# A routed mixture of experts on one core: seven single tiles for eight, an earlier index table, and third tiles in column groups

## The chip, the cores and the metric

The kernel runs on one core of one Trainium2 chip. The metric is the device time of one execution in microseconds (us), taken as the median of several runs; lower is better.

## The reference

There are 64 x 64 = 4096 tokens of 256 numbers. Each token goes to two of eight experts, and the experts' outputs, scaled by softmax weights, are added to the token. Cut to what matters:

```python
var = jnp.mean(x * x, axis=-1, keepdims=True)
xn = rms_w * (x * jax.lax.rsqrt(var + EPS))
gate = xn @ wg_W + wg_b + (genre_embed @ gg_W + gg_b)        # [64, 64, 8]
gate_w = jax.nn.softmax(gate, axis=-1)
topk_w, topk_i = jax.lax.top_k(gate_w, 2)
cw = jnp.sum(jax.nn.one_hot(topk_i, E) * topk_w[..., None], axis=-2)
h1 = jax.nn.relu(jnp.einsum('bsh,ehm->bsem', x, W1) + b1)     # 256 -> 512
h2 = jax.nn.relu(jnp.einsum('bsem,emn->bsen', h1, W2) + b2)   # 512 -> 512
out_e = jnp.einsum('bsen,enh->bseh', h2, W3) + b3             # 512 -> 256
x = x + jnp.einsum('bseh,bse->bsh', out_e, cw)
```

All is float32. The kernel computes only the two chosen experts of each token: 8192 pairs of token and expert.

## The kernel before

**Two routings.** A token's number is 32 p + i; the tokens with i under 8 (`NA`, 1024 tokens) are the first part. `first_part` finds their experts early. Each expert's first 128 pairs of this part form a *single*, a tile of 128 rows, units u = 0 to 7 (`E`). While the singles run, the generator `rest` routes all else: it counts for every expert how many pairs are left (`mm`), gives each its tiles of 128 rows (`nb_i`) and its number of blocks of 32 rows (`ints`), chooses the shape of the tail, and computes for each row of the rest which token it holds. That last step is a table: VectorE builds one-hot matrices in four chunks (L774, L776, L779, the buffers `ohl`, `ohh`, `ohv`), and 64 small matmuls in float16 (`table`, L613) add them up in PSUM bank 7; from it VectorE makes the indices `idxR` (L785 to L788). `gather_unit` then lets GpSimd gather the rows of x for the first two units of the rest.

**The rest's units.** A unit holds up to four tiles of one expert; its width counts blocks of 32 rows, at most 16. `SHAPES` lists 32 tails (q, p, widths) that the program holds as separate code: q units of width 16, then the experts' last units, of which p come with a unit of width 8 behind them. At the run the first listed shape that fits is jumped to; if none fits, a general one. For the inputs here, by the counts of the reference's routing, it is (5, 6, (15, 14, 12, 11, 11, 10, 16, 9)): five units of 16, then 16, 9, 15, 8, 14, 8, 12, 8, 11, 8, 11, 8, 10, 8. Expert 7 has 300 pairs in the first part and 945 behind it; with 128 in its single, 1117 are left, 35 blocks.

**How a unit is computed.** A single runs `layer1` (L1043, 8 matmuls), `layer2` (L1053, 16) and `layer3` (L1290, 4 of 256 columns), each float32 matmul showing as two records. Units of more than one tile use a fast scheme with seven products in place of eight (`Fast` for layers 1 and 2, L1152; `Wide` for layer 3, L1254), named p(1) to p(7); VectorE makes the sums (`mix`, `c11`, `c12`, `c22`) and ScalarE copies and relus. Layer 3 in that scheme takes tiles by twos, so a unit of three tiles computes its third tile's layer 3 with plain matmuls (L1290), whatever its number of rows.

**The order.** It is written by hand; engines work their instructions in the order of the program, waiting on semaphores. `head_step(u)` is the order around single u: layer 1 of u, the transposes of u + 1, layer 3 of u - 1, layer 2 of u, and calls of `more(ns)`, which put some of the rest's routing at that place. `step` does the same for the last single, and `step_fast` for the units of the rest: layers 1 and 2 of unit u with the end of layer 2 and layer 3 of unit u - 1 between them. `give(u)` scales the result on VectorE (L1321) and adds the rows into the output with a scatter on GpSimd (L1322); a unit's scatters wait until those of the unit before have landed. The output is filled with x ahead of that by four copies (`fill`, SP's queue). `pB.spread` makes the weights of the second routing on GpSimd (L432 to L434) and stores them in DRAM (`cwdR`, L435), `gather_cw` gathers them for a unit (`cg`), and `scales` copies the expert's column (`cw`, L1014). The weights come from DRAM on SP's queue: `load_weights` for the singles' layers 1 and 3 (rings of three buffers, `w1r` and `w3r`) and all experts' layer 2 (`w2a`), `stream_1` and `stream_3` for the rest's units.

Of the kernel before, what the change touches and what calls it, by code (L numbers as in the profile page):

```python
# [58 lines left out]
def kernel(  # L59
# [38 lines left out]
    NREST = (NPAIR - TOPK * BT + E * (BT - 1)) // BT  # L98
    NSURE = (NPAIR - E * BT) // BT
# [515 lines left out]
    def rest():  # L615
# [41 lines left out]
        V.tensor_tensor(totA, totA1[:, 1:], totA1[:, 0:E], ALU.subtract)  # L657
        V.tensor_scalar(more, totA, float(-BT), 0.0, ALU.add, ALU.max)
# [73 lines left out]
        V.scalar_tensor_tensor(pA.slot, pA.slot, float(-BT), pA.along(base), ALU.add, ALU.add)  # L732
        for k, sum_ in enumerate((place, turn_e)):
# [1007 lines left out]
```

## Time and profile before

| what | value |
| --- | --- |
| median of 3 runs | 451.8 us (451.03 to 452.44) |
| the profiled execution | 451.29 us, its span 449.6 us |
| TensorE (PE) busy | 440.6 us, 98% of the span |
| VectorE (DVE) busy | 358.3 us, 80% |
| ScalarE (ACT) busy | 258.3 us, 57% |
| GpSimd (POOL) busy | 274.7 us, 61% |
| read from and written to memory | 56.34 MB and 20.12 MB |

The span runs from the first to the last instruction. A row of a timeline gives start and duration in us, engine, line, operation, output and input tile, the shapes and how many in a row; in brackets stands how long the engine stood idle before it and what ended that. Matmuls overlap, so what a group of them costs is read from its start to the start of the next, not from its duration. The singles run from 22 to 87 us, the units of the rest behind that.

### The profile page before, as it was taken

Reading aid. Unit: us, or ns where it says so; the run is one execution under the profiler, and the core shown is the slowest. Engines: PE = TensorE matmul, PEld = TensorE weight load, DVE = VectorE, ACT = ScalarE, POOL = GpSimd, SP = SyncE. Lnnn points to the kernel's source line nnn. Section 1 sums busy time; section 2 is a strip of 40 time slices with the busy share of each in tenths; the row PEclk is TensorE's granted clock in tenths of the full one; section 3 lists DMA queues with packets and bytes.
Section 4 is the critical chain, followed back from the end, with each engine's and each line's share of the span. In section 5 each row is a group of like instructions: output and inputs, shape, how many; then the busy total and the mean of one; then the engine's idle time right before and its main releaser. Section 6 shows DMA issues by size and latency. Waiting matters only on the chain.

```text
span 449.6 us, 9495 instructions
## 1 busy us (share of the span) xinstructions
PE 440.6 (98%) x3092; PEld 414.6 (92%) x3092; DVE 358.3 (80%) x988; ACT 258.3 (57%) x618; POOL 274.7 (61%) x234
## 2 busy tenths in 40 slices
PE   8899999999999999999999999999999999999994
PEld 7689999988989899999999899999999999999994
DVE  5797995677798888888899877977977878779851
ACT  6755543456465555646475655755755765666642
POOL 4355522857888875737475864874775766667333
PEclk9999999999999999999999999999999999999998
DMA  8799999794666757545654563474464565555213
GB/s 292 277 330 372 378 372 383 279 251 91 186 158 150 164 87 195 94 115 106 145 117 100 92 156 96 68 166 106 66 163 108 124 132 117 123 107 105 25 16 41
DMA packets 71599, 72.51 MB, mean 161 GB/s; under 512 B 34735, under 2 KB 60818, under 8 KB 71156
## 3 DMA queue, kind: packets, MB, share of 16 engines
q1 hardware_dynamic: 48976, 43.29, 30.9%
q0 software_dynamic: 14960, 17.50, 23.0%
q10 hardware_dynamic: 7604, 11.02, 7.9%
q8 instruction: 26, 0.43, 0.4%
q14 instruction: 33, 0.27, 0.2%
HBM read 56.34 MB, written 20.12 MB: 170 GB/s over the span
## 4 chain that ended last, share of the span: by engine, by line
PE 90%; DMA 3%; DVE 2%; issue 1%; POOL 1%; POOLq 0%; SPq 0%; DVEq 0%
PE pb L1152 54%; PE pb L1254 18%; PE pb L1053 6%; PE pb L1290 5%; PE pb L1043 3%; DMA big<-in_x_dram 2%; POOL out_dram L1322 1%; PE pb L613 1%; PE pb L934 1%; DMA xg<-in_x_dram,idxA 1%; PE pb L253 1%; DVE xT L922 0%; DVE big L1129 0%; POOLq L1641 0%; PE pb L271 0%
## 5 line engine op out<-in xcount | busy, mean ns | idle before, releaser
L1322 POOL DMA_INDIRECT out_dram<-ys,idxR x57 | 98.8, 1732 | 81.7 <-DVE ys L1321 64.1
L1152 PE MATMUL pb<-hid,big 128*128 128x256 f32 (+7 forms) x456 | 83.0, 325 | 0.0
L1173 ACT ACTIVATE hid<-hid,bb 128x256 f32<-128x256 f32 (+12 forms) x154 | 72.9, 523 | 12.6 <-DVE hid L1167 12.3
L867 POOL DMA_INDIRECT cg<-cwdR,idxR x59 | 64.0, 1085 | 18.0 <-issue 17.7
L1152 PEld LDWEIGHTS pb<-hid,big 128*128 128x128 f32 x456 | 70.4, 191 | 3.4
L1161 ACT COPY big<-pb 128x512 f32<-128x512 f32 (+7 forms) x57 | 27.2, 477 | 64.8 <-PE pb L1152 46.6
L1152 PE MATMUL pb<-mixB,big 128*128 128x256 f32 (+7 forms) x304 | 55.5, 325 | 0.1
L1152 PE MATMUL pb<-hotA,big 128*128 128x256 f32 (+7 forms) x304 | 55.3, 325 | 0.0
L1152 PEld LDWEIGHTS pb<-mixB,big 128*128 128x128 f32 x304 | 47.9, 191 | 3.1 <-ACT bc L1031 0.5
L1152 PEld LDWEIGHTS pb<-hotA,big 128*128 128x128 f32 x304 | 46.6, 191 | 2.1
L1152 PE MATMUL pb<-mixX,iotx 128*128 128x256 f32 (+7 forms) x228 | 46.5, 327 | 0.0
L867 POOL DMA_INDIRECT big<-in_x_dram,idxR x32 | 36.0, 1124 | 9.8 <-issue 8.5
L867 POOL DMA_INDIRECT xgE<-in_x_dram,idxR x27 | 30.9, 1145 | 16.1 <-issue 15.2
L1152 PEld LDWEIGHTS pb<-mixX,iotx 128*128 128x128 f32 x228 | 36.6, 191 | 2.9 <-issue 0.8
L1161 ACT COPY q1s<-pb 128x512 f32<-128x512 f32 (+7 forms) x57 | 26.9, 472 | 19.0 <-PE pb L1152 17.6
L1275 DVE TENSOR_TENSOR ys<-pb,big 128x128 f32<-128x128 f32 (+1 forms) x54 | 18.7, 347 | 22.3 <-PE pb L1254 15.4
L1263 ACT COPY big<-pb 128x128 f32<-128x128 f32 (+1 forms) x54 | 16.7, 309 | 25.9 <-PE pb L1254 25.9
L1053 PEld LDWEIGHTS pb<-hid,w2a 128*128 128x128 f32 x256 | 29.8, 192 | 1.1 <-issue 0.8
L1152 PE MATMUL pb<-xT,w1r 128*128 128x256 f32 (+7 forms) x152 | 30.8, 325 | 0.0
L1053 PE MATMUL pb<-hid,w2a 128*128 128x128 f32 x256 | 30.5, 276 | 0.0
L922 DVE STREAM_TRANSPOSE xT<-gTs 128x256 f32<-128x256 f32 x55 | 29.3, 638 | 0.5 <-DMA gTs<-scr 0.5
L1031 ACT ACTIVATE bc<-b_sb,cw 128x256 f32 x59 | 26.1, 499 | 6.1 <-DVE cw L1014 5.0
(340 smaller groups left out, 925.5 us busy)
## 6 DMA issues: line engine op xcount, KB each, us to landing
w2a<-in_L_cond_W_dram SPq DMA_DIRECT2D x8, 1024.0 KB, 13.2
w1r<-in_L_cond_W_dram SPq DMA_DIRECT2D x11, 512.0 KB, 11.5
w3r<-in_L_cond_W_dram ACTq DMA_DIRECT2D x11, 512.0 KB, 3.9
w3r<-in_L_cond_W_dram SPq DMA_DIRECT2D x10, 512.0 KB, 12.9
w1r<-in_L_cond_W_dram ACTq DMA_DIRECT2D x10, 512.0 KB, 3.8
gTs<-scr SPq DMA_DIRECT2D x7, 512.0 KB, 4.3
out_dram<-in_x_dram SPq DMA_DIRECT2D x4, 768.0 KB, 9.5
scr<-big SPq DMA_DIRECT2D x5, 512.0 KB, 4.3
```

Of the source, the lines that this page charges most:

```text
L867: return nc.gpsimd.indirect_dma_start(out=dst, out_offset=None, in_=src, in_offset=bass.IndirectOffsetOnAxis(ap=index(b), axis=0), bounds_ ...
L922: V.transpose(xT[:, :, s0 + k, :].rearrange("p c (b k) -> p k c b", b=SQ), shs[:, s0 + k].rearrange("p k (a c) -> p k c a", a=SQ),)
L1031: nc.scalar.mul(bc, b3e, cw)
L1053: nc.tensor.matmul(ph, lhsT=w2[:, m, ts(n, P)], rhs=hid[0][:, m, 0:BT], start=(m == 0), stop=(m == MC - 1))
L1152: nc.tensor.matmul(bank[:, ts(n, self.w)], lhsT=w[:, c, ts(n, P)], rhs=x[:, c], start=new and n == 0 and c == 0, stop=n == HB - 1 and c == ...
L1161: nc.scalar.copy(self.q[(1, 6, 5).index(k)], self.tall(self.X if k == 5 else self.U))
L1173: nc.scalar.activation(out, src, AF.Relu, bias=ww[self.u][1][:, self.l, n : n + 1])
L1254: nc.tensor.matmul(bank[:, ts(j, H // 2)], lhsT=a[:, c, ts(j, P)], rhs=b[:, c], start=new and j == 0 and c == 0, stop=j == self.n - 1 and ...
L1263: nc.scalar.copy(self.q[(1, 6, 5).index(k)], self.X if k == 5 else self.U)
L1275: V.tensor_tensor(self.y(j, i), src, self.q[q].rearrange("p (k h) -> p k h", k=self.n), ALU.add)
L1290: nc.tensor.matmul(sums(u, k)[0 : cols.stop - cols.start], lhsT=hid[1][:, n, cols], rhs=w3[:, n, :], start=(i == 0), stop=(i == MC - 1),)
L1322: add = nc.gpsimd.indirect_dma_start(out=orows, out_offset=bass.IndirectOffsetOnAxis(ap=index(b)[0:n], axis=0), in_=y[0:n], in_offset=None ...
```

## The change

`F = 7` takes the place of `E` where singles are counted. Expert 7 has no single: its pairs of the first part go into the rest, so it has 1245 pairs there, 39 blocks, and the shape chosen is (5, 6, (15, 15, 14, 12, 11, 10, 16, 9)), from a new list. Its layer 1 and layer 3 weights are no longer loaded for a single. The table's last matmuls, the indices and the gathers come one single earlier, ahead of layer 2 of single 5, and all that follows them moves with them. A third tile of at most 64 rows (`strip`) puts its four products into column groups of TensorE, side by side on PSUM's partitions (`third_tile`), and adds the groups with a matmul against a 0/1 matrix (`join`; `both`, and `four` for 32 rows). `r1`, a relu on ScalarE, moves behind the third tile.

The diff, cut to its core (the other places only put `F` for `E`; of the 32 shapes the one that is used is shown):

```diff
 SHAPES = [
-    (5, 6, (15, 14, 12, 11, 11, 10, 16, 9)),
+    (5, 6, (15, 15, 14, 12, 11, 10, 16, 9)),
...
-    NREST = (NPAIR - TOPK * BT + E * (BT - 1)) // BT
-    NSURE = (NPAIR - E * BT) // BT
+    F = 7
+    NREST = (NPAIR - max(F - E + TOPK, 0) * BT + E * (BT - 1)) // BT
+    NSURE = (NPAIR - F * BT) // BT
...
-        V.tensor_tensor(totA, totA1[:, 1:], totA1[:, 0:E], ALU.subtract)
-        V.tensor_scalar(more, totA, float(-BT), 0.0, ALU.add, ALU.max)
+        V.tensor_tensor(more, totA1[:, 1:], totA1[:, 0:E], ALU.subtract)
+        V.tensor_scalar(more[:, 0:F], more[:, 0:F], float(-BT), 0.0, ALU.add, ALU.max)
...
-        V.scalar_tensor_tensor(pA.slot, pA.slot, float(-BT), pA.along(base), ALU.add, ALU.add)
+        V.tensor_scalar(low, pA.slot[:, 0:F], float(BT), float(-4 * NPAIR - BT), ALU.is_lt, ALU.mult)
+        V.tensor_tensor(pA.slot, pA.slot, pA.along(base), ALU.add)
...
+        V.scalar_tensor_tensor(pA.slot[:, 0:F], pA.slot[:, 0:F], float(-BT), low, ALU.add, ALU.add)
...
-        V.tensor_tensor(sl[:, :, 0:NA], sl[:, :, 0:NA], low, ALU.add)
...
     def sums(u, k):
 
         if size(u) == 3 and k == 2:
-            return PB[2][:, 0:H]
+            return PB[2][:, H : 2 * H] if strip(u) and u not in ends else PB[2][:, 0:H]
...
+    def strip(u):
+
+        rows = width(u) - 2 * BT
+        return rows if size(u) == 3 and rows <= BT // 2 else 0
+
+    def third_tile(u):
+
+        r = strip(u)
+        if not r:
+            layer3(u, [2])
+            return
+        w3, c0 = ww[u][3], 2 * BT
+        ways = P // r
+        for n in range(MC):
+            q = n % ways
+            nc.tensor.matmul(
+                PB[2][q * r : (q + 1) * r, 0:H],
+                lhsT=hid[1][:, n, c0 : c0 + r],
+                rhs=w3[:, n, :],
+                start=n < ways,
+                stop=n >= MC - ways,
+                skip_group_check=True,
+            )
+        nc.scalar.copy(ring(run, [P, H], "xg", 3, 0), PB[2][:, 0:H])
+
+    def join(u):
+
+        r = strip(u)
+        if r:
+            fold = both if r == BT // 2 else four
+            nc.tensor.matmul(PB[2][0:r, H : 2 * H], lhsT=fold, rhs=ring(run, [P, H], "xg", 3, 0), start=True, stop=True)
...
     def head_step(u, more):
...
-        table(GC * (NCH - 1) * (u == E - 2))
         layer1(u)
         if u + RING < E:
-            load_weights(u + RING, (0, 1))
+            load_weights(u + RING, (0, 1) if u + RING < F else (1,))
...
-            if u == E - 2:
-                while not fetched:
-                    more(1000000)
+            if u == F - 2:
+                more(1000000)
             elif u != 2:
                 more(3200)
             scaled(u - 1, "A")
             layer3(u - 1)
...
-        table(GC * (u == E - 3))
+        table(GC * (u == F - 2))
...
-        if u == E - 2:
-            stream_3(E, mybir.EngineType.SP)
+        if u == F - 2:
             fill(2)
-            stream_1(E + 1, mybir.EngineType.SP)
-            stow(E + 1)
-            shuffle(E + 1)
-            fill(3)
             give(u - 2)
-        if u >= 1 and u != E - 3:
+        if u >= 1 and u != F - 3:
             give(u - 1)
...
     def step(u, last):
 
         far = fetches_of(u, last)
+        if u == F - 1:
+            while not fetched:
+                next(other)
+            stream_3(F, mybir.EngineType.SP)
+            stream_1(F + 1, mybir.EngineType.SP)
+            stow(F + 1)
+            shuffle(F + 1)
+            fill(3)
...
+        if u == F - 1:
+            for _ in other:
+                pass
...
-            elif u + 1 == E:
-                for l in (1, 0):
-                    for _ in Fast(E, l).fold():
+            elif u + 1 == F:
+                for l in (0, 1):
+                    for _ in Fast(F, l).fold():
                         pass
...
             third.p(1)
-            f.r1()
             third.p(2)
             if n == 3:
-                layer3(u - 1, [2])
+                third_tile(u - 1)
+            f.r1()
...
             if n == 3:
+                join(u - 1)
                 give(u - 1, [2])
...
-        for u in range(E - 1):
+        for u in range(F - 1):
             head_step(u, routing)
-        for _ in other:
-            pass
-        for u in range(E - 1, CUT):
+        V.tensor_tensor(four, both[:, 0 : P // 4], both[:, P // 4 : P // 2], ALU.add)
+        for u in range(F - 1, CUT):
```

What this moves, engine by engine. On TensorE, around the end of single 5 (`xT` and `w1r` layer 1, `w2a` layer 2, `w3r` layer 3, `pb_75<-big` the table; the table's rows repeat 16 times a chunk and are cut), before:

```order
L1043 MATMUL pb_71<-xT,w1r_84 128x128 x2
L934 MATMUL pb_72<-ident,xg_205 128x128 x2
L1290 MATMUL pb_73<-w3r_87,hid_91 128x256 x4
L613 LDWEIGHTS big
L613 MATMUL pb_75<-big 128x69
...
L1053 MATMUL pb_68<-hid_90,w2a 128x128 x4
```

And now:

```order
L1043 MATMUL pb_71<-xT,w1r_84 128x128 x2
L934 MATMUL pb_72<-ident,xg_205 128x128 x2
L615 LDWEIGHTS big
L615 MATMUL pb_75<-big 128x70
...
L1322 MATMUL pb_73<-w3r_87,hid_91 128x256 x4
...
L1053 MATMUL pb_68<-hid_90,w2a 128x128 x4
```

Before, 16 of the table's matmuls stand between layer 3 of single 4 and layer 2 of single 5, and 48 further down (32 ahead of layer 1 of single 6, 16 behind it). Now 16 stand ahead of that layer 3 and the other 48 behind it, all ahead of layer 2 of single 5.

On GpSimd, from the last gathers of singles (`xg`) to the first weights of the rest (`cg`); `out_dram` is a `give`'s scatter, before:

```order
L867 DMA xg_206<-in_x_dram,idxA 128x256
L1322 DMA out_dram<-ys,idxA 4096x256
L867 DMA xgE<-in_x_dram,idxR 128x256 x4
L867 DMA big<-in_x_dram,idxR 128x256 x4
L802 COPY cw8B<-cw8A 128x64
...
L435 DMA cwdR<-cw8B 128x256
L1322 DMA out_dram<-ys,idxA 4096x256
L1322 DMA out_dram<-xg_207,idxA 4096x256
L867 DMA cg<-cwdR,idxR 128x8 x4
L1322 DMA out_dram<-xg_205,idxA 4096x256
```

And now:

```order
L1354 DMA out_dram<-ys,idxA 4096x256
L867 DMA big<-in_x_dram,idxR 128x256 x4
L867 DMA xgE<-in_x_dram,idxR 128x256 x4
L1354 DMA out_dram<-ys,idxA 4096x256
L1354 DMA out_dram<-xg_206,idxA 4096x256
L802 COPY cw8B<-cw8A 128x64
...
L437 DMA cwdR<-cw8B 128x256
L867 DMA cg<-cwdR,idxR 128x8 x4
L1354 DMA out_dram<-xg_207,idxA 4096x256
```

The scatters of singles 3 and 4, of which the first stood ahead of the gathers and the second behind the store of `cwdR`, now both stand between the gathers and the copy that begins the spread; the `cg` gathers come right behind the store.

On VectorE, at the routing's one-hot chunks (`big<-iotx`, `big<-whole`, `big<-big,xgE`), before:

```order
L774 TENSOR_TENSOR big<-iotx,lo_854 128x2048
L776 TENSOR_TENSOR big<-whole,hi_855 128x1104
L779 TENSOR_TENSOR big<-big,xgE 128x1104
L1321 SCALAR_TENSOR_TENSOR ys<-pb_74,cg,bc_574 128x256
L774 TENSOR_TENSOR big<-iotx,lo_854 128x2048
```

And now:

```order
L779 TENSOR_TENSOR big<-big,xgE 128x1120
L785 TENSOR_SCALAR sa<-pb_75 128x70
...
L795 SCALAR_TENSOR_TENSOR nex<-ia,fit,ib 128x1
L1353 SCALAR_TENSOR_TENSOR ys<-pb_74,cg,bc_574 128x256
L1353 SCALAR_TENSOR_TENSOR xg_206<-pb_73,cg,bc_571 128x256
```

The `give` of single 3 stood between the first two chunks and now stands behind the indices, beside that of single 4.

More of the change, by code (lines that the diff above doesn't have):

```diff
@@ L169 @@
     nc.gpsimd.tensor_tensor(both, ident[:, 0 : P // 2], ident[:, P // 2 : P], ALU.add)
+    four = const.tile([P, P // 4], F32, name="four")
     fresh = const.tile([P, NB, E], F32, name="fresh")
@@ L644, in rest @@
         place, turn_e = t2("place", 1), t2("turn_e", 1)
+        sl, low = buf(gx, [P, TOPK, NI], "sl"), buf(gx, [P, F, NA], "low")
         flat = pin.rearrange("p a k e -> p a (k e)")
@@ L788, in rest @@
         V.tensor_tensor(idxR, sa, sb, ALU.add)
-        gather_unit(E)
-        gather_unit(E + 1)
+        gather_unit(F)
+        gather_unit(F + 1)
         total, ia, ib = ends[:, KE - 1 : KE], t2("ia", 1), t2("ib", 1)
@@ L830, in width @@
     def width(u):
-        return BT if u < E else SQ * plan[u - E][1]
+        return BT if u < F else SQ * plan[u - F][1]
     def group(u):
-        return u if u < E else E + plan[u - E][2]
+        return u if u < F else F + plan[u - F][2]
     def follow(u):
-        return u > E and group(u) == group(u - 1)
+        return u > F and group(u) == group(u - 1)
     def size(u):
@@ L845, in tiles @@
     def tiles(u):
-        b = u if u < E else E + plan[u - E][0]
+        b = u if u < F else F + plan[u - F][0]
         return list(range(b, b + size(u)))
     def turn_of(u, k):
-        return (u if u < E else E + sum(size(v) for v in range(E, u))) + k
+        return (u if u < F else F + sum(size(v) for v in range(F, u))) + k
     def within(u, k):
@@ L862, in index @@
     def index(b):
-        return idxA[:, b : b + 1] if b < E else idxR[:, b - E : b - E + 1]
+        return idxA[:, b : b + 1] if b < F else idxR[:, b - F : b - F + 1]
     def fetch(dst, src, b):
@@ L895, in gather_cw @@
             cg = cgs[b] = cgR[:, turn_of(u, k) % NCG]
-            fetch(cg, (cwdA if b < E else cwdR)[:, :], b)
+            fetch(cg, (cwdA if b < F else cwdR)[:, :], b)
     xT = buf(run, [P, HC, SLOTS, BT], "xT")
@@ L932, in transpose_x @@
             for k, b in enumerate(bs):
-                g = ring(run, [P, H], "xg", 3, b) if u < E else xgR[u % 2][:, k]
+                g = ring(run, [P, H], "xg", 3, b) if u < F else xgR[u % 2][:, k]
                 nc.tensor.transpose(tps[c][:, ts(k, BT)], g.rearrange("p (r c) -> p c r", c=HC)[:, c], ident)
-            if u == E:
+            if u == F:
                 (nc.scalar.copy if c else V.tensor_copy)(
@@ L985, in streams @@
     def streams(u, end):
-        if E < u + 2 < end and not follow(u + 2):
+        if F < u + 2 < end and not follow(u + 2):
             stream_1(u + 2)
-        if E < u + 1 < end and not follow(u + 1):
+        if F < u + 1 < end and not follow(u + 1):
             stream_3(u + 1)
     def stage_1(u):
-        if u < E:
+        if u < F:
             ww[u] = [w1r[u % RING], vT[:, :, u, :], w2a[:, u], w3r[u % RING]]
@@ L1019, in scaled @@
         cws = []
-        e = expert(u, mybir.EngineType.Activation) if eng == "A" and u >= E else ex.get(u)
+        e = expert(u, mybir.EngineType.Activation) if eng == "A" and u >= F else ex.get(u)
         for k, b in enumerate(tiles(u)):
@@ L1330, in give @@
             )
-            if b < E:
+            if b < F:
                 for f in fills[1:]:
-                    tc.declare_no_dep(add.ins, f.ins, reason="the first E tiles hold tokens of the first part alone")
+                    tc.declare_no_dep(add.ins, f.ins, reason="the first F tiles hold tokens of the first part alone")
             behind = list(adds[-2]) if len(adds) > 1 else [fills[0]]
-            if b >= E and not behind_fills:
+            if b >= F and not behind_fills:
                 behind += fills[1:]
@@ L1358, in head_step @@
     def head_step(u, more):
-        if u + 3 < E:
+        if u + 3 < F:
             gather(u + 3)
-        for k in range(3 * u, min(3 * u + 3, E)):
+        for k in range(3 * u, min(3 * u + 3, F)):
             gather_cw(k)
-        table(GC * (NCH - 1) * (u == E - 2))
         layer1(u)
         if u + RING < E:
-            load_weights(u + RING, (0, 1))
+            load_weights(u + RING, (0, 1) if u + RING < F else (1,))
         if u == 0:
@@ L1410, in fill @@
         for a in sum(adds, []):
-            tc.declare_no_dep(f.ins, a.ins, reason="the first E tiles hold tokens of the first part alone")
+            tc.declare_no_dep(f.ins, a.ins, reason="the first F tiles hold tokens of the first part alone")
         fills.append(f)
     def fetches_of(u, last):
-        far = E + 1 < u + 2 < last
+        far = F + 1 < u + 2 < last
         if far:
@@ L1431, in step @@
         if len(ww[u - 1]) < 5:
-            if u - 1 >= E:
+            if u - 1 >= F:
                 scales(u - 1)
@@ L1456, in step @@
         layer3(u - 1)
-        if u == E - 1:
-            stream_1(E + 2, mybir.EngineType.SP)
-            stream_3(E + 1, mybir.EngineType.SP)
+        if u == F - 1:
+            stream_1(F + 2, mybir.EngineType.SP)
+            stream_3(F + 1, mybir.EngineType.SP)
         give(u - 1)
     def step_fast(u, last):
-        if u == E:
+        if u == F:
             transpose_x(u)
@@ L1473, in step_fast @@
         n = size(u - 1)
-        e = expert(u, mybir.EngineType.Activation) if u > E and not follow(u) else None
+        e = expert(u, mybir.EngineType.Activation) if u > F and not follow(u) else None
         fresh_w, fold_next = not follow(u), fast_next and not follow(u + 1)
-        if u == E:
+        if u == F:
             layer3(u - 1, part=(0, 1))
@@ L1573, in step_fast @@
             shuffle(u + 2)
-        small = u > E
+        small = u > F
         if small:
@@ L1653, in steps @@
                 nc.gpsimd.drain()
-    CUT = E + NQT - 2
+    CUT = F + NQT - 2
     ENGS = (
@@ L1706 @@
         plan[:] = ARMS[k]
-        last = E + len(plan)
+        last = F + len(plan)
         with tc.manual_schedule():
```

38 lines of the change are left out of this document (17 added, 21 removed), and 60 rows, old and new, of the table SHAPES.

## The prediction

> **What bounds the kernel now.** I read the page first, then who waits for whom on TensorE, then the timelines of TensorE, VectorE and GpSimd around the places that the change touches.
>
> ```profile
> span 449.6 us, 9495 instructions
> PE 440.6 (98%) x3092; PEld 414.6 (92%) x3092; DVE 358.3 (80%) x988; ACT 258.3 (57%) x618; POOL 274.7 (61%) x234
> ```
> ```profile
> PE pb L481 <- DVE ones L158: 1.1, 1, 1.1
> PE pb L253 <- DMA big<-in_x_dram: 0.8, 1, 0.8
> PE pb L934 <- DMA xg<-in_x_dram,idxA: 0.6, 1, 0.6
> ```
>
> The first fence is the page's head, the second all that TensorE waits for: 2.5 us, all before 22 us. So TensorE (PE) is the bound: its work counts in full, and every wait put into its queue counts in full. The question is whether the shorter head puts waits there.
>
> **The single that goes.** The last single's layers stand undisturbed in TensorE's timeline (start, duration; from one start to the next is what a group costs):
>
> ```profile
> 63.27 0.40 PE L934 MATMUL pb<-ident,xg 128*128 128x128 f32 x2
> 63.51 1.89 PE L1290 MATMUL pb<-w3r,hid 128*128 128x256 f32 x8
> 65.24 1.14 PE L613 MATMUL pb<-big 128*128 128x69 f16 x16
> 66.20 3.82 PE L1053 MATMUL pb<-hid,w2a 128*128 128x128 f32 x32
> ...
> 80.27 1.95 PE L1043 MATMUL pb<-xT,w1r 128*128 128x128 f32 x16
> 82.06 1.89 PE L1290 MATMUL pb<-w3r,hid 128*128 128x256 f32 x8
> 83.78 3.73 PE L1053 MATMUL pb<-hid,w2a 128*128 128x128 f32 x32
> 87.36 1.12 PE L934 MATMUL pb<-ident,xgE 128*128 128x128 f32 x8
> ```
>
> Layer 1 costs 82.06 - 80.27 = 1.79, layer 3 83.78 - 82.06 = 1.72, layer 2 87.36 - 83.78 = 3.58, and a single's transposes 63.51 - 63.27 = 0.24: 7.33 us less. Its weights' loads (1 MB for layers 1 and 3), its gathers and its scatter lay beside other work and no wait hung on them: nothing.
>
> **The rows that come back.** Expert 7's 128 pairs of the first tokens now join its rest: 1117 pairs become 1245, 35 blocks of 32 become 39. Its last unit grows from width 11 to 15, and the units run 15, 8, 15, 8, 14, 8, 12, 8, 11, 8, 10, 8 where they ran 15, 8, 14, 8, 12, 8, 11, 8, 11, 8, 10, 8. One "11 and 8" becomes a "15 and 8". Layer 1 of a unit begins with these rows; half the width in elements is the moving side (224 is width 14, 192 is 12, 176 is 11), and the next two are from the grouped view, mean ns of one:
>
> ```profile
> 283.41 0.92 PE L1152 MATMUL pb<-xT,w1r 128*128 128x224 f32 x4
> 318.06 0.82 PE L1152 MATMUL pb<-xT,w1r 128*128 128x192 f32 x4
> 349.07 0.76 PE L1152 MATMUL pb<-xT,w1r 128*128 128x176 f32 x4
> 378.95 0.76 PE L1152 MATMUL pb<-xT,w1r 128*128 128x176 f32 x4
> ```
> ```profile
> L1152 PE MATMUL pb<-hid,big 128*128 128x240 f32 x24 | 5.4, 366 | 0.0
> L1152 PE MATMUL pb<-hid,big 128*128 128x224 f32 x24 | 5.0, 353 | 0.0
> ```
>
> "14 and 8" takes 318.06 - 283.41 = 34.65, "11 and 8" 378.95 - 349.07 = 29.88. From 14 to 15 each of the 84 records (7 products x 2 x 3 matmuls, two records each) takes 366 - 353 = 13 ns more, 1.10 us; layer 3 is the same for four tiles. So 15 and 8 is 35.75, and the change adds 5.87 us. The additional tile's gather, scale and scatter run on GpSimd, 61% busy: nothing, as long as that engine keeps ahead; behind they would cost 1 to 2 us each.
>
> **Column groups.** Third tiles of 32 and 64 rows (the units of width 9 and 10) put their four products beside each other and sum them in one more matmul. The nearest rows are four matmuls of 512 columns in groups of 32, which the gates already do, and the third tile of 32 rows as it is:
>
> ```profile
> 25.11 1.46 PE L284 MATMUL pb<-big,wg_sb 128*32 128x512 f32 x8
> 26.51 0.71 PE L1053 MATMUL pb<-hid,w2a 128*128 128x128 f32 x4
> ```
> ```profile
> 252.42 1.91 PE L1290 MATMUL pb<-w3r,hid 128*32 128x256 f32 x8
> 254.27 1.08 PE L1152 MATMUL pb<-mixX,iotx 128*128 128x240 f32 x4
> ```
>
> One after another, four of 512 columns would take 2 x 1.73 = 3.46 us (63.51 to 65.24 is four of 256); they took 1.40, so groups do run together: two passes of 0.43 and 0.54 for going in and out of the narrow shape. With 256 columns that is 0.43 + 0.54 = 0.97 for four groups and 0.86 + 0.54 = 1.40 for two. The sum over groups is one matmul of 256 columns, 1.73 / 4 = 0.43, and 0 to 0.54 for the shape again. Width 9 goes from 1.85 to between 1.40 and 1.94; width 10, one after another now at some 1.85 too, to between 1.83 and 2.37. Together -0.5 to +0.6; I take -0.3, nearer to the lower end because the narrow tile pays for its shape today as well, partly ahead of the 1.85. The Trainium skill (TensorEngine Tiling (Array Packing), Overview) gives up to 4x for 32 rows and 2x for 64; by that the two third tiles with their sums would take 0.86 and 1.29, and the change would be worth 1.5 us here, 1.2 more than I take. The same page's section Tiling Modes says that a change of mode drains the array, which the 0.54 of this trace bears out. The later relu (`r1`, now behind the third tile) stays on ScalarE, 57% busy: nothing.
>
> So TensorE's work changes by -7.33 + 5.87 - 0.3 = -1.76 us. Now the waits.
>
> **First wait: the table.** The 64 one-hot matmuls that give the rest's indices stood 16 behind layer 3 of single 4, 32 before layer 1 of single 6, 16 behind it. Now all stand before layer 2 of single 5. VectorE makes their operands without a pause from 46 us on:
>
> ```profile
> 61.13 0.48 DVE L1321 SCALAR_TENSOR_TENSOR ys<-pb,cg,bc 128x256 f32<-128x256 f32 x1
> 61.53 1.21 DVE L774 TENSOR_TENSOR big<-iotx,lo 128x2048 f16<-128x2048 f16 x1
> ...
> 70.24 0.73 DVE L779 TENSOR_TENSOR big<-big,xgE 128x1104 f16<-128x1104 f16 x1
> 75.09 0.23 DVE L785 TENSOR_SCALAR sa<-pb 128x69 f32<-128x69 f32 x1 [4.12 <-PE pb L613]
> 75.76 0.23 DVE L788 TENSOR_TENSOR idxR<-sa,sb 128x69 int32<-128x69 f32 x1
> ```
>
> The last operand ends at 70.97. One `give` (61.13 to 61.53) moves behind it: 70.57; the other edits of the routing (a wider `low`, one operation less, 1120 columns for 1104) cancel to 0.1. TensorE reaches the last 16 early: transposes done at 63.51, 16 table matmuls 0.96, layer 3 1.73, 32 more 1.92, so 68.1. It waits until 70.6, some 2.5 us. Before, VectorE waited there (4.12). TensorE then reaches the rest's first transposes at 87.36 - 7.33 + 2.5 = 82.5, 4.8 us earlier than now. The indices come 3.3 us earlier (70.6 + 1.14 = 71.8 where 75.09 stood), so the gathers that those transposes need have 1.5 us less of their cover; nothing in the trace waits there now, and I put up to 0.5 us on it, which the next wait swallows. On SP's queue the rest's first weights and the copies of x to the output go out about a single earlier, past nothing that waits, and 1 MB shorter: nothing. VectorE's folds of the rest's first weights start with layer 1's now and fit between the indices and 82.5.
>
> **Second wait: the scales.** GpSimd, in order, issued eight gathers, the weights' spread and its store, two scatters of singles, and then the scales' gathers (`cg`); the second scatter waits until the first has landed. Now both scatters stand ahead of the spread, so the store waits for a landed scatter, and the `cg` gathers for the store:
>
> ```profile
> 22.54 0.63 POOL L435 DMA_DIRECT2D cwdA<-cw8A  x1 [0.29 <-POOL cw8A L434]
> ...
> 29.31 1.10 POOL L867 DMA_INDIRECT cg<-cwdA,idxA  x1 [3.27 <-DMA cwdA<-cw8A]
> ...
> 87.73 0.26 POOL L802 COPY cw8B<-cw8A 128x64 f32<-128x64 f32 x1
> 90.27 0.64 POOL L435 DMA_DIRECT2D cwdR<-cw8B  x1 [0.30 <-POOL cw8B L434]
> 91.21 1.64 POOL L1322 DMA_INDIRECT out_dram<-ys,idxA  x1 [0.30 <-DVE mixX L1135]
> 96.95 1.84 POOL L1322 DMA_INDIRECT out_dram<-xg,idxA  x1 [4.09 <-DVE hotA L1135]
> 99.09 1.21 POOL L867 DMA_INDIRECT cg<-cwdR,idxR  x1 [0.30 <-issue]
> ```
> ```profile
> 105.60 0.15 DVE L1014 COPY cw<-cg 128x1 f32 x1 [1.19 <-DMA cg<-cwdR,idxR]
> 106.29 0.68 DVE L1170 TENSOR_TENSOR hid<-pb,big 128x512 f32<-128x512 f32 x1
> ```
> ```profile
> 108.44 1.89 PE L1152 MATMUL pb<-mixB,big 128*128 128x256 f32 x8
> ```
>
> The eight gathers end at 87.73 - 3.3 = 84.4. The first scatter goes at 84.7, the second 5.74 later as between 91.21 and 96.95 (VectorE, named there, had long been done: it is the landing), 90.4; its issue 1.84, the spread 90.27 - 87.73 = 2.54, and the store starts at 94.8. From store to first `cg`: at most 29.31 - 22.54 = 6.77, as with the first part's store under full weight loads, at least the 2.5 us in which a `cg` gather lands (median, page, last column):
>
> ```profile
> cg<-cwdR,idxR POOLq DMA_INDIRECT x59, 2.5
> out_dram<-ys,idxR POOLq DMA_INDIRECT x57, 4.3
> ```
>
> I take 4.0, nearer to the lower end since the weight loads are thinner by then: 98.8. The last scale reaches VectorE 105.60 - 99.09 = 6.5 later, 105.3, and the sum behind it (L1170) ends 1.37 later (106.29 + 0.68 - 105.60), 106.7. TensorE's product at 108.44 overwrites what that sum reads. Its slack is 108.44 - 106.97 = 1.47 now; it would be due at 108.44 - 4.8 = 103.6 and waits 3.1 us (1.6 to 5.9 by the bounds of the store).
>
> So from there on TensorE is 108.44 - 106.7 = 1.75 us earlier than now, where the removed work alone gave 7.33. The sum: -1.75 + 5.87 - 0.3 = +3.8 us. Between the bounds of the store it is +2.3 to +6.6. The profiled execution took 451.29 us for its span of 449.6; with 3.8 it is 455.1. The median of the runs, 451.8, lies 0.5 above that execution; I stay with 455.1 and let the range take the difference.
>
> **Rivals.**
> - Only the table's wait shows, the `cg` chain hides (chance 0.15). It decides if the last scale lands by 102.2 (103.6 less 1.37), 3.1 earlier than I have it: the first scatter would have to land in some 4 us and the store in 2.5. For it: 4.3 us as the usual landing of a scatter (the row above). Against it: the 5.74 between these very scatters, and that VectorE waits for the last `cg` already now (1.19). It gives -1.76 + 2.5 = +0.7 us, 452.0.
> - No wait shows at all, so faster (0.08). It needs VectorE's last operand by 68.1, 2.5 us earlier than the sum has it, and the `cg` chain hidden too: the whole of the row's chain from 46 us on would have to be shorter. Against it: VectorE's timeline has no gap there from which 2.5 us could come. It gives 451.29 - 1.76 = 449.5.
> - The stalled array comes back at a lower clock (0.07). The trace has no wait of over 1.1 us in TensorE (the second fence), so it cannot show this. A wait as long as my second, 3.1 us, and then as long at half speed would add some 1.6: 456.7. The Trainium skill (TensorE: Matmul & The Clock Gate, Part 1) states this rule, with a window of about 3.4 us that must be idle; my first wait is under it, the second at its edge.
> - Column groups do not run together for these tiles (0.05): four matmuls one after another, the sum and the shape, 0.43 to 0.97 more for each of the two units where I take 0.3 less: +1.7 on my sum, 456.8. Against it: the 1.40 above.
>
> **How the numbers follow.** My case has 0.65: 455.1, with 453.6 to 457.9 as its own range by the bounds of the store. A measurement of this kernel tells about 0.3%, 1.4 us, from no change. Slower by more than that: my case, the clock and the groups, 0.77. Within it: the first rival, 0.15. Faster: 0.08. For 8 in 10 the range reaches down to the first rival with some of its spread, 451.0, and up to 457.3, where the last part of the store's bound and of the clock's case stays out.
>
> **What would show it.** TensorE waiting some 2 us for VectorE before the last table matmuls (L615) near 68 to 71 us, and 2 to 4 us for VectorE's L1170 (its line is the same) near 103 to 107; VectorE there waiting for `cg` for 4 us or more; on GpSimd two scatters between the eighth gather and the copy of `cw8B`; TensorE's busy time 1.5 to 2.5 us smaller; a unit of width 15 where one of 11 stood. A `cg` chain that lands early, or a VectorE that reaches the table's end before TensorE, would prove me wrong, and the time would be at or under 452.0.

## The result and the profile after

The changed kernel takes 457.0 us (median of 6 runs, 455.55 to 457.38), the kernel before on the same chip 451.5 (451.03 to 452.44): a ratio of 1.0108, 95% interval 1.0092 to 1.0124, some 5 us slower. The profiled execution took 456.85 us, 1.75 over the forecast 455.1. A ratio, here and below, leaves out executions more than 1.5% above the fastest of their kernel, among them three of 1170, 1608 and 1667 us, and is not quite the quotient of the two medians.

The page's head and what TensorE waits for, in the changed kernel (columns: us in total, times, longest):

```profile
span 455.1 us, 9414 instructions
PE 441.6 (97%) x3058; PEld 414.7 (91%) x3058; DVE 363.2 (80%) x991; ACT 257.1 (56%) x611; POOL 270.9 (60%) x234
```
```profile
PE pb L615 <- DVE big L779: 2.7, 2, 2.0
PE pb L1152 <- DVE xT L936: 1.7, 1, 1.7
```

TensorE does less work, and yet its busy time is 1.0 us longer. Its timeline shows why:

```profile
68.27 1.14 PE L615 MATMUL pb<-big 128*128 128x70 f16 x16 [0.64 <-DVE big L779]
71.42 1.16 PE L615 MATMUL pb<-big 128*128 128x70 f16 x16 [2.01 <-DVE big L779]
72.39 6.29 PE L1053 MATMUL pb<-hid,w2a 128*128 128x128 f32 x32
78.52 1.95 PE L1043 MATMUL pb<-xT,w1r 128*128 128x128 f32 x16
...
89.25 1.13 PE L1152 MATMUL pb<-xT,w1r 128*128 128x256 f32 x4 [1.67 <-DVE xT L936]
...
108.61 1.89 PE L1152 MATMUL pb<-mixB,big 128*128 128x256 f32 x8
```

The table's wait is there (0.64 and 2.01 us). Behind it layer 2 of single 5 takes 78.52 - 72.39 = 6.13 us; that of single 6, in the same trace, takes 3.57 (82.03 to 85.60). The view by stretches of 2 us gives the granted clock, the third number from the end of a row (1.00 is full speed):

```profile
70.00:72.00 2.00, 0.58 (x10) 0.58 (x10) 1.33 (x2) 0.00 (x0) 0.00 (x0) 0.69 1.06 396
72.00:74.00 2.00, 2.00 (x17) 2.00 (x16) 1.25 (x8) 0.00 (x0) 0.00 (x0) 0.50 1.08 406
...
78.00:80.00 2.00, 2.00 (x21) 2.00 (x20) 0.00 (x0) 1.32 (x4) 1.42 (x2) 1.00 1.07 391
```

The clock was at half (0.50) until some 77.5 us, and TensorE counts as busy while it works at half speed: so less work shows as more busy time. Then TensorE waits 1.67 us for xT. VectorE's and ScalarE's timelines show what is late:

```profile
81.22 0.35 DVE L428 TENSOR_REDUCE denB<-wB 128x24 f32<-128x192 f32 x1 [6.24 <-ACT wB L422]
...
87.52 0.68 DVE L1110 TENSOR_TENSOR big<-big 128x512 f32<-128x512 f32 x1
...
88.52 0.68 DVE L936 COPY xT<-pb 128x512 f32<-128x512 f32 x1
```
```profile
79.22 1.71 ACT L1046 ACTIVATE hid<-pb,vT 128x128 f32<-128x128 f32 x4
80.83 0.35 ACT L422 ACTIVATE wB<-wB 128x192 f32<-128x192 f32 x1
```

VectorE stood idle for 6.24 us: the exponentials (L422) stand on ScalarE behind the relus of single 6's layer 1, which TensorE reached late. The folds and xT stand behind them. Last, the chain of the scales, on GpSimd and on VectorE:

```profile
85.03 1.68 POOL L1354 DMA_INDIRECT out_dram<-ys,idxA  x1 [0.30 <-issue]
89.80 1.58 POOL L1354 DMA_INDIRECT out_dram<-xg,idxA  x1 [3.09 <-DVE mixX L1135]
...
93.84 0.65 POOL L437 DMA_DIRECT2D cwdR<-cw8B  x1 [0.30 <-POOL cw8B L436]
99.53 1.08 POOL L867 DMA_INDIRECT cg<-cwdR,idxR  x1 [5.04 <-DMA cwdR<-cw8B]
```
```profile
106.44 0.15 DVE L1014 COPY cw<-cg 128x1 f32 x1 [1.82 <-DMA cg<-cwdR,idxR]
...
107.13 0.68 DVE L1170 TENSOR_TENSOR hid<-pb,big 128x512 f32<-128x512 f32 x1
```

L1170 ends at 107.81, and TensorE's product behind it starts at 108.61 without a wait, since TensorE is late already. Before, it started at 108.44. So of the 7.33 us that the head lost in work, nothing is left at this place: 2.65 (table) + 2.56 (clock) + 1.67 (xT) = 6.88, 0.2 from the start of the program, and some 0.4 beside the waits, where a group takes up to 0.2 us more from start to start than its work and its wait together (68.27 to 71.42 is 3.15 for 0.96 and 2.01).

### The profile page after: what moved, and what is told of

It is laid out like the page before. It is cut to its first block, busy times and chain, and to the rows that moved or that the text cites. A ratio compares the mean times of both kernels' runs of the same rounds, so it can differ in the third digit from the quotient of the medians.

```text
span 455.1 us, 9414 instructions
## 1 busy us (share of the span) xinstructions
PE 441.6 (97%) x3058; PEld 414.7 (91%) x3058; DVE 363.2 (80%) x991; ACT 257.1 (56%) x611; POOL 270.9 (60%) x234
## 4 chain that ended last, share of the span: by engine, by line
PE 83%; DVE 10%; issue 2%; POOL 1%; DMA 1%; ACT 1%; POOLq 0%; DVEq 0%; ACTq 0%
PE pb L1152 55%; PE pb L1254 18%; PE pb L1053 3%; PE pb L1322 2%; PE pb L1043 1%; DVE big L776 1%; POOL out_dram L1354 1%; PE pb L483 1%; DVE big L774 1%; PE pb L255 1%; DVE big L779 1%; PE pb L286 1%; DMA xg<-in_x_dram,idxA 1%; DVE ys L1353 1%; DVE xT L922 0%
## 5 line engine op out<-in xcount | busy, mean ns | idle before, releaser
L1354 POOL DMA_INDIRECT out_dram<-ys,idxR x58 | 96.8, 1670 | 84.4 <-DVE ys L1353 69.5
L1152 PE MATMUL pb<-hid,big 128*128 128x256 f32 (+7 forms) x456 | 84.5, 329 | 0.0
L867 POOL DMA_INDIRECT cg<-cwdR,idxR x60 | 67.1, 1119 | 23.0 <-issue 17.1
L1152 PEld LDWEIGHTS pb<-hid,big 128*128 128x128 f32 x456 | 71.2, 191 | 4.4 <-ACT hid L1173 0.8
L1152 PE MATMUL pb<-mixB,big 128*128 128x256 f32 (+7 forms) x304 | 56.3, 328 | 0.2 <-DVE hid L1170 0.2
L1152 PE MATMUL pb<-hotA,big 128*128 128x256 f32 (+7 forms) x304 | 56.2, 328 | 0.0
L1152 PEld LDWEIGHTS pb<-mixB,big 128*128 128x128 f32 x304 | 48.5, 191 | 3.4 <-ACT bc L1031 0.5
L1152 PEld LDWEIGHTS pb<-hotA,big 128*128 128x128 f32 x304 | 47.1, 191 | 2.3
L1152 PE MATMUL pb<-mixX,iotx 128*128 128x256 f32 (+7 forms) x228 | 47.2, 329 | 0.0
L867 POOL DMA_INDIRECT xgE<-in_x_dram,idxR x33 | 36.8, 1114 | 10.1 <-issue 8.8
L867 POOL DMA_INDIRECT big<-in_x_dram,idxR x27 | 29.5, 1093 | 20.8 <-PE pb L1053 12.9
L1152 PEld LDWEIGHTS pb<-mixX,iotx 128*128 128x128 f32 x228 | 36.8, 191 | 3.0 <-issue 0.8
L1275 DVE TENSOR_TENSOR ys<-pb,big 128x256 f32<-128x256 f32 (+1 forms) x54 | 19.2, 355 | 25.4 <-PE pb L1254 19.2
L1152 PE MATMUL pb<-xT,w1r 128*128 128x256 f32 (+7 forms) x152 | 31.3, 329 | 1.7 <-DVE xT L936 1.7
L1053 PEld LDWEIGHTS pb<-hid,w2a 128*128 128x128 f32 x224 | 28.6, 207 | 1.0 <-issue 0.8
L1053 PE MATMUL pb<-hid,w2a 128*128 128x128 f32 x224 | 29.3, 292 | 0.0
L1173 ACT ACTIVATE hid<-pb,bb 128x256 f32<-128x256 f32 (+7 forms) x76 | 27.8, 417 | 2.3 <-PE pb L1152 1.8
```

Of the source, the lines that this page charges most:

```text
L867: return nc.gpsimd.indirect_dma_start(out=dst, out_offset=None, in_=src, in_offset=bass.IndirectOffsetOnAxis(ap=index(b), axis=0), bounds_ ...
L1053: nc.tensor.matmul(ph, lhsT=w2[:, m, ts(n, P)], rhs=hid[0][:, m, 0:BT], start=(m == 0), stop=(m == MC - 1))
L1152: nc.tensor.matmul(bank[:, ts(n, self.w)], lhsT=w[:, c, ts(n, P)], rhs=x[:, c], start=new and n == 0 and c == 0, stop=n == HB - 1 and c == ...
L1173: nc.scalar.activation(out, src, AF.Relu, bias=ww[self.u][1][:, self.l, n : n + 1])
L1275: V.tensor_tensor(self.y(j, i), src, self.q[q].rearrange("p (k h) -> p k h", k=self.n), ALU.add)
L1354: add = nc.gpsimd.indirect_dma_start(out=orows, out_offset=bass.IndirectOffsetOnAxis(ap=index(b)[0:n], axis=0), in_=y[0:n], in_offset=None ...
```

## The experiments

Theory A: three limits lie one behind the other (the table with its clock, the exponentials with xT, the scales at L1170), and who removes one only reaches the next. Theory B: they add, and each is worth its own size. Two landmarks in TensorE's timeline are read from each trace: the start of the product behind L1170, and that of the first L1254 behind it, where layer 3 of the first unit of the rest begins. Both are from one profiled execution, the median is over four or more. Medians of different calls compare through the kernel before, which ran in each (451.5 to 452.1).

| kernel | median, us | ratio to before (95%) | product | L1254 |
| --- | --- | --- | --- | --- |
| before | 451.5 | 1 | 108.44 | 112.76 |
| changed | 457.0 | 1.0108 (1.0092 to 1.0124) | 108.61 | 112.93 |
| exponentials early | 457.3 | 1.0105 (1.0083 to 1.0127) | 108.23 | 114.33 |
| table behind layer 2 | 458.0 | 1.0147 (1.0117 to 1.0178) | 107.99 | 112.41 |
| wait filled | 457.6 | 1.0113 (1.0081 to 1.0146) | 107.53 | 113.64 |
| gives first | 454.0 | 1.0044 (1.0026 to 1.0062) | 105.83 | 110.15 |
| fills later | 457.9 | 1.0134 (1.0119 to 1.0149) | 105.68 | 111.79 |
| table between | 456.9 | 1.0121 (1.0101 to 1.0141) | 105.59 | 111.59 |
| fills behind scales | 460.5 | 1.0182 (1.0157 to 1.0208) | 102.15 | 106.46 |
| groups alone | 451.2 | 0.9982 (0.9972 to 0.9992) | 108.66 | 112.98 |

**Four runs on a disturbed chip.** The first four kernels ran where the kernel before itself took 464.8 to 480.1 us, with stalls that the other traces do not have (in three of the four TensorE waits 4.8 to 13.5 us in all for ScalarE's copies at L1263, in no other trace at all); their ratios say nothing of 1%. Two of them were run again (below); their first ratios were 1.0182 (1.0079 to 1.0285) for the exponentials early and 1.0175 (1.0066 to 1.0284) for the table behind layer 2. The other two were the exponentials with the spread ahead of the scatters,

> The exponentials as in the run before, and the spread of the weights with the store of cwdR ahead of the two scatters of singles 3 and 4 on GpSimd. The store then starts near 87.8 us (93.84 now); the second scatter still waits for the first to land, so the gathers of cg start at 95.3 to 96.3 (99.53 now) and L1170 ends by 103.6 to 104.6. Theory A: the chain of the scales no longer limits, the wait of 1.67 us for xT is gone too, and nothing takes their place: 1.7 us less, 455.2 for a profiled execution of 456.85, some 0.9 us less than with the exponentials alone. Theory B: also 1.7 us less, but no difference to the exponentials alone.

(ratio 1.0111, 0.9892 to 1.033), and all three edits together,

> All three edits: layer 2 of single 5 ahead of the table's last 48 matmuls, the exponentials right behind it, the spread with its store ahead of the two scatters. Theory A: the chain of the scales ends at L1170 by 104.1 to 105.1 us, the gathers land near 82, and TensorE reaches the product behind L1170 at 104 to 105 (108.61 now): 3.5 to 4.6 us less, 452.3 to 453.4 for a profiled execution, far more than the parts alone give together (0.8 or 1.7 and 0). Theory B: the parts add, 5.2 + 1.7 = 6.9 us less, 450.0.

(1.0148, 1.003 to 1.0267). Neither decides anything. The second showed one thing, TensorE's row at layer 3 of single 5 (L1321 and L1352 are L1322 and L1353 of the changed kernel):

```profile
81.96 1.99 PE L1321 MATMUL pb<-w3r,hid 128*128 128x256 f32 x8 [0.99 <-DVE ys L1352]
```

It waits for single 3's give, which VectorE had behind the weights; hence the order of a later run.

**The exponentials alone.**

```diff
         fetched.append(F)
-        yield None
         pB.exps()
+        yield None
```

> The changed kernel with the exponentials alone moved, again, since its first run fell on a chip with disturbed transfers. Theory A: the wait of 1.67 us for xT goes, but L1170 still ends near 107.8 and the product behind it, due at 106.9, waits 0.8 to 0.9 us: 456.1 for a profiled execution. Theory B: 455.2 and no new wait. For comparison the fill of the first wait, which brought TensorE 3 us earlier at p(1), came out at 457.6 in the median, not faster than the changed kernel.

```profile
85.82 1.03 PE L1152 MATMUL pb<-xT,w1r 128*128 128x256 f32 x4
...
108.23 3.34 PE L1152 MATMUL pb<-mixB,big 128*128 128x256 f32 x8 [2.98 <-DVE hid L1170]
111.36 1.41 PE L1152 MATMUL pb<-xT,w1r 128*128 128x256 f32 x4
112.61 1.03 PE L1152 MATMUL pb<-mixX,iotx 128*128 128x256 f32 x4
```

The wait for xT is gone, p(1) starts 3.4 us earlier (1.3 of it because layer 2 of single 5 took 4.9 us here), and TensorE then waits 2.98 us for L1170. The two groups behind that wait take 112.61 - 108.23 = 4.38 us in place of 1.73 + 0.86, so 1.8 us go to the clock. A, not B: at the product 0.4 us are left. A left out the clock behind the new wait.

One trace shows one execution. Of the four of this kernel two took 455.9 and 456.3 us, where A had put it, and two 458.2 and 458.3; the trace is one of the longer. The next two kernels part in the same way: 456.2 and 456.6 (the trace is the 456.2) against 459.5 and 460.0, then 455.9 and 456.1 against 459.2 and 459.5 (the trace is the 459.2). In the short trace the wait for L1170 costs 0.1 us of clock, in the two long ones 1.8. So the clock behind that wait may be part of what separates the executions; with one trace of each kernel that is not shown.

**Layer 2 ahead of the table.**

```diff
+        elif u == F - 2:
+            layer2(u)
+            more(3200)
         else:
             more(3200)
             layer2(u)
```

> The same kernel as the run with layer 2 of single 5 ahead of the table's last 48 matmuls, whose first run fell on a chip with disturbed transfers. Theory A, limits one behind the other: the two waits for VectorE (2.65 us) and the low clock (2.56 us) go, but TensorE then waits for the first gathers and for xT, and behind that for L1170, which ends near 108.3: a profiled execution of 456.6 to 457.2 (456.85 for the changed kernel). Theory B, waits add: 451.6.

```profile
69.71 3.12 PE L615 MATMUL pb<-big 128*128 128x70 f16 x48
72.66 2.03 PE L1043 MATMUL pb<-xT,w1r 128*128 128x128 f32 x16
...
81.29 0.39 PE L934 MATMUL pb<-ident,big 128*128 128x128 f32 x1 [0.93 <-DMA big<-in_x_dram,idxR]
82.42 2.40 PE L934 MATMUL pb<-ident,big 128*128 128x128 f32 x7 [0.74 <-DMA big<-in_x_dram,idxR]
84.60 1.77 PE L1322 MATMUL pb<-w3r,hid 128*128 128x256 f32 x4
86.21 1.03 PE L1152 MATMUL pb<-xT,w1r 128*128 128x256 f32 x4
...
107.99 1.99 PE L1152 MATMUL pb<-mixB,big 128*128 128x256 f32 x8 [2.36 <-DVE hid L1170]
```

Both waits and the low clock before 78 us are gone, TensorE is 5.9 us ahead at layer 1 of single 6 (72.66 for 78.52), and 0.6 us of it are left at the product. The next limits took the place: the first gathers hold TensorE for 0.93 and 0.74 us, and the clock falls behind these two as well (0.50 from 84 to 86 us). The seven transposes take 84.60 - 82.42 = 2.18 us where eight took 0.95 in the changed kernel, the part of layer 3 behind them 86.21 - 84.60 = 1.61 for 0.87 in the kernel before; some 2.1 us are lost together. Then comes L1170 with 2.36. The profiled execution took 456.23 us (B said 451.6), and the median is no better than the changed kernel's. This is the plainest of the runs: the largest loss was taken away whole, and 0.6 us came of it.

**The wait filled.** Is it the wait that lowers the clock, or the table's light float16 matmuls?

```diff
         yield None
+        table(2 * GC)
+        busy(5)
+        table(3 * GC)
+        busy(16)
         table()
```

> The changed kernel with 5 and 16 transposes of the identity, whose result nobody reads, put into TensorE's two waits of 0.64 and 2.01 us before the table's last 32 matmuls; nothing else is moved. If the waits lowered the clock: it stays at 1.00, layer 2 of single 5 takes 3.6 us (6.13 in the changed kernel) and ends 2.5 us earlier. If the light float16 matmuls of the table did it: 0.5 to 0.7 as in the changed kernel, and layer 2 takes 6 us. For the time, theory A (limits one behind the other): the 2.5 us carry to p(1), at 86.7, but L1170 still ends near 107.8, where the product behind it would be due at 106.1, so only 0.7 to 0.9 us come off, 456.0 for a profiled execution. Theory B: 2.5 us, 454.3.

```profile
71.83 3.82 PE L1057 MATMUL pb<-hid,w2a 128*128 128x128 f32 x32
75.49 1.95 PE L1047 MATMUL pb<-xT,w1r 128*128 128x128 f32 x16
...
107.53 3.62 PE L1156 MATMUL pb<-mixB,big 128*128 128x256 f32 x8 [1.87 <-DVE hid L1174]
110.94 1.13 PE L1156 MATMUL pb<-xT,w1r 128*128 128x256 f32 x4
```
```profile
72.00:74.00 2.00, 2.00 (x19) 2.00 (x19) 1.82 (x10) 0.41 (x2) 0.29 (x1) 1.00 1.06 419
109.00:111.00 2.00, 2.00 (x7) 1.55 (x6) 1.91 (x5) 1.27 (x2) 1.70 (x2) 0.50 0.34 113
```

(L1047, L1057, L1156 and L1174 are L1043, L1053, L1152 and L1170.) With the same table the clock stays at 1.00 and layer 2 takes 3.66 us: it was the waits, not the table's matmuls. 1.1 us of the 2.5 are left at the product, which waits 1.87 us for L1170, and half the clock behind it takes 1.8 more. This execution lost another 1.5 us at a wait of 0.86 us for ScalarE (L1165) at 161.70 us, which no trace of the other kernels in the table shows, so its 459.16 is no measure of the edit. The shorter two of four, 455.9 and 456.1, are where A had put it (456.0), and none came near B's 454.3.

**Scales first, and the fills.** The next kernels take away several limits at once. In all, layer 2 stands ahead of the table, the exponentials and the spread stand behind it, ahead of the scatters, single 3's and 4's gives right behind the indices, and single 4's scatter behind the gathers of cg:

```diff
+            give(u - 2, do="V")
+            give(u - 1, do="V")
+            more(3200)
+            give(u - 2, do="S")
```

> Layer 2 of single 5 ahead of the table's last 48 matmuls, the exponentials behind that layer, and the spread with its store ahead of the scatters. Added to what was tried before: VectorE scales the results of singles 3 and 4 right behind the indices, and the scatter of single 4 stands behind the gathers of cg. Theory A: the first gathers land near 81.8 us, so p(1) starts near 83.2 (89.25 in the changed kernel); the store of cwdR starts near 88, cg's gathers at 93.6, L1170 ends near 101.9, before TensorE's product at 102.6 needs it: about 6.0 us less than the changed kernel, 450.8 for a profiled execution. Theory B: 2.65 + 2.56 + 1.67 = 6.9 us less, 450.0; the two lie close here, and the trace decides by whether TensorE waits for the gathers (A: about 1.8 us).

```profile
81.66 0.39 PE L934 MATMUL pb<-ident,big 128*128 128x128 f32 x1 [1.43 <-DMA big<-in_x_dram,idxR]
82.82 1.36 PE L934 MATMUL pb<-ident,big 128*128 128x128 f32 x7 [0.77 <-DMA big<-in_x_dram,idxR]
84.02 1.73 PE L1322 MATMUL pb<-w3r,hid 128*128 128x256 f32 x4
85.54 1.91 PE L1152 MATMUL pb<-xT,w1r 128*128 128x256 f32 x4
...
105.83 1.89 PE L1152 MATMUL pb<-mixB,big 128*128 128x256 f32 x8
```

3 us less than the changed kernel, where A said 6: nothing waits at L1170 any more, but the gathers held TensorE for 2.2 us and the clock behind them cost some 2 more (84.02 to 85.54 is 1.52 for 0.86). While the gathers were under way the DMA engines were busy throughout (share 1.03 from 76 to 80 us), the output's fills among what they moved. So the second to fourth fill were issued at 94.5 us:

> As the run with the results of singles 3 and 4 scaled first, and the output's second to fourth fill (1 KB rows of x, 0.75 MB each) issued behind the weights of the second and third unit of the rest, some 95 us, and not between 66 and 71. In that run TensorE waited 2.2 us for the first gathers, which landed 3 to 6.7 us after their issue while the DMA engines were busy all the time until 82 us, and then ran 2 us at a lower clock. Theory C, the fills delay the gathers: the gathers land about 3 us after issue as later in the program, the fourth near 81.8; TensorE waits 1 to 1.5 us in place of 2.2, the clock stays or falls for shorter, p(1) starts at 83.3 to 84.5 (85.54 in that run) and the scales' chain stays ahead of it: 1 to 2.2 us less than that run's 454.0, so 451.8 to 453.0. Rival: the gathers' delay is GpSimd's own and the fills do not matter: 454.0 as that run.

```profile
81.96 0.87 PE L934 MATMUL pb<-ident,big 128*128 128x128 f32 x5 [1.23 <-DMA big<-in_x_dram,idxR]
...
105.68 2.52 PE L1152 MATMUL pb<-mixB,big 128*128 128x256 f32 x8 [2.72 <-DVE hid L1170]
```
```profile
100.00:104.00 4.00, 2.96 (x14) 2.27 (x12) 0.31 (x2) 1.30 (x3) 0.26 (x1) 1.00 1.03 399
```

C holds for the gathers (the DMA share from 76 to 80 us is 0.56, the wait 1.23 us, p(1) at 83.54, 2.0 us earlier), but the time is worse than C's 451.8 to 453.0: the fills now load the DMA engines just when cg's gathers should land (share 1.03 from 100 to 104, 0.37 in the run before), and L1170 is the limit again. With the table between the quarters of layer 2 it is the same, 0.5 us earlier at p(1) and a wait of 3.12 us at L1170, so that the rival named below came true and not the 450.0 to 450.5:

```diff
-            layer2(u)
-            more(3200)
+            layer2(u, {0: lambda: table(2 * GC), 1: lambda: table(3 * GC), 2: lambda: more(3200)})
```

> As the run with the fills later, and the table's last 48 matmuls go in groups of 16 between the quarters of layer 2 of single 5, so that the last group starts when VectorE ends its operands (70.9 us) and not 2 us behind. Indices and gathers then come 1.0 us earlier at the same work of TensorE. Theory A with C: the wait for the first gathers shrinks to 0.3 us or so, the clock stays at 1.00, p(1) starts near 82.4 to 82.8 and the product behind L1170 near 102.0: 6.4 to 6.8 us less than the changed kernel, 450.0 to 450.5 for a profiled execution, at or just under the kernel before with its column groups (451.0). Rival, the scales' chain takes over again at L1170: at or above 451.5.

The last run put the fills behind the store of the third unit's rows:

> As the run with the table between the quarters of layer 2, and the output's second to fourth fill moved once more: on SP's queue behind the store of the third unit's gathered rows (near 112 us), so that they load the DMA engines neither when the first gathers land (75 to 82 us) nor when cg's gathers do (92 to 100 us). Theory A with C: the last cg lands by about 100.5 us, L1170 ends by 101.9, TensorE's product behind it is due at 102.3 and waits 0 to 0.5 us, the clock stays at 1.00: 450.5 to 451.3 for a profiled execution, 5.5 to 6.3 us less than the changed kernel, and level with the kernel before with its column groups (451.2). Rival: the scales' chain is slow by itself, not by the fills: L1170 ends at 103.5 to 105.6 as in the last runs and the time is 453 to 456.

```profile
102.15 1.89 PE L1152 MATMUL pb<-mixB,big 128*128 128x256 f32 x8
...
130.42 2.07 PE L1152 MATMUL pb<-xT,w1r 128*128 128x256 f32 x4 [7.18 <-DVE xT L922]
132.29 3.62 PE L1152 MATMUL pb<-hid,big 128*128 128x256 f32 x8
135.70 1.08 PE L1152 MATMUL pb<-mixX,iotx 128*128 128x256 f32 x4
```
```profile
129.29 1.99 DVE L922 STREAM_TRANSPOSE xT<-gTs 128x256 f32<-128x256 f32 x4 [10.14 <-DMA gTs<-scr]
```

Up to 123 us A with C is right to 0.2 us: the product at 102.15 (102.3 expected), 6.3 us before that of the kernel before, so most of the 7.33 can be had at this place. Then the fills delay gTs, the third unit's transposed rows, and TensorE waits 7.18 us and loses 2.7 more to the clock (1.01 at p(1), 1.68 at the product behind it). The load of gTs stands behind the three fills on the same queue, SP's, so this run does not tell whether it waited for the queue or for busy DMA engines; the gathers of cg are on GpSimd's queue, and there it cannot be the queue's order. Without this one wait and its clock it would be 460.57 - 9.9 = 450.7, an estimate and a best case, since a next limit may stand behind it: a place for the fills that harms nobody was not run. Even 450.7 is level with the profiled execution of the column groups alone (450.92, next), for the removed single is worth 7.33 - 5.87 = 1.46 us at most.

**The column groups alone**, with eight singles as before:

```diff
-                layer3(u - 1, [2])
+                third_tile(u - 1)
+            f.r1()
```

> The kernel before with the column groups alone (third tiles of 32 and 64 rows, the join, and r1 behind them), eight singles as before. My term for them was -0.3 us (-0.5 to +0.6); by the starts in the trace of the changed kernel it is -0.5 for the width of 9 and about -0.3 for that of 10, so -0.6 to -0.9 us and 450.4 to 450.7 for a profiled execution (451.29 before). If groups of columns did not run together, or r1 came late for its reader, it would be +0.5 or more.

```profile
252.64 0.64 PE L1300 MATMUL pb<-w3r,hid 128*32 128x256 f32 x8
253.21 1.08 PE L1153 MATMUL pb<-mixX,iotx 128*128 128x240 f32 x4
...
255.11 0.62 PE L1315 MATMUL pb<-xg,four 128*32 128x256 f32 x2
255.66 1.89 PE L1153 MATMUL pb<-hid,big 128*128 128x240 f32 x8
```

Four groups take 253.21 - 252.64 = 0.57 us where the third tile took 1.85, the join 255.66 - 255.11 = 0.55 more. The ratio is 0.9982, 0.8 us less than before (0.4 to 1.3), as expected. Of all that was run this is the one version that beats both kernels: 451.2 us.

## Why the prediction was right, and where it failed

- **The removed single and the width.** Right. The second "15 and 8" costs 318.88 - 283.11 = 35.77 us by the starts of its first products in the changed kernel, 35.75 in the sum.
- **The column groups.** Mis-sized: -0.8 us (0.4 to 1.3 less) for -0.3, in the middle outside of -0.5 to +0.6. I charged 0.54 for going in and out of the narrow shape beside the pass of 0.43; four groups took 0.57 in all, which leaves 0.14. So these rows do not bear out the 0.54 as the price of such a visit.
- **The first wait.** Right in place and size: 2.65 us for 2.5.
- **The clock.** The step that failed most. I gave it 0.07 and only behind the second wait. It came behind the first, for 2.56 us. The run with the wait filled shows that it was the wait. The rule on which I called the first wait too short is that of the Trainium skill (TensorE: Matmul & The Clock Gate, Part 1), an idle window of about 3.4 us. It does not fit here: 0.64 and 2.01 us, with 1 us of the table between, were enough.
- **"VectorE's folds fit between the indices and 82.5".** Wrong. I followed VectorE's queue and not ScalarE's: the exponentials had moved behind layer 1 of single 6, and xT came 1.67 us late.
- **The scales' chain.** The mechanism was right: two scatters ahead of the spread, L1170 at 107.81 (106.7 forecast). The store took 5.7 us to the first `cg`, not 4.0. But the wait of 3.1 us that I put there did not show, since the clock and xT had used up the same time before. The runs that took those away found it at once, 1.87 to 2.98 us.
- **The signs.** The table's wait, the place of the two scatters and the unit of width 15 were there. Three signs were not: TensorE did not wait for L1170, VectorE's longest wait for `cg` was 1.82 us and not 4, and TensorE's busy time grew by 1.0 us where it should have fallen by 1.5 to 2.5.
- **The sum.** At the product behind L1170 I had -1.75, it was +0.17; that is the whole miss of 1.9 us in that term. +0.17 + 5.87 - 0.8 = 5.2, the span grew by 5.5; of the 0.3 between, 0.2 is a wait for L1170 at 248.06 us that the kernel before does not have, the rest I did not trace.

So that the time came out near the forecast is partly luck: the clock and xT, 2.56 + 1.67 = 4.23 us that I had put at nothing, stand where I had 3.1 us of waiting for L1170. The direction was safer than the sum. Without the wait for xT, or without the low clock, or without the table's wait and its clock, L1170 held the product at 107.5 to 108.2 us, about where it was before.

## What to carry to other kernels

When work is taken from the engine that bounds a kernel, walk every queue that feeds it, not only the one that waits first: each of the three edits that took away one limit alone brought 0.4 to 1.1 us at the product behind L1170, that for the largest loss (5.2 us) 0.6. Where TensorE waits, look at the granted clock behind the wait: it cost from nothing to 2.7 us more here. A bulk transfer with nobody waiting for it is not free: it must lie where no small gather is awaited.

## What the hardware showed that I had not expected

Waits of TensorE and the time lost behind them to the clock, by the starts of the rows behind the wait against the same rows at full clock:

- 0.96, 1.23 and 1.67 us lost nothing, 2.36 lost 0.1.
- 1.87, 2.72 and 2.98 us lost 1.8 each, 3.12 lost 1.7, and 7.18 lost 2.7.
- 2.01 us alone lost 1.3, and 2.56 with a wait of 0.64 us ahead of it.
- Two short waits close together did it too: 0.93 and 0.74 us lost some 2.1, 1.43 and 0.77 about 2.

So when the clock fell it cost 1.3 to 2.7 us, much the same behind 1.87 us of waiting as behind 3.12, and the length of one wait does not decide whether it falls. The Trainium skill (TensorE: Matmul & The Clock Gate, Part 1) says that the window of activity runs free of the program, which would allow such scatter; no run here shows the window itself.
